# LayerNorm outputs transposed once in float32 and split behind the transpose, in a fused attention and ternary-FFN kernel

## The chip, the cores and the metric

The kernel runs on one core of one Trainium2 chip. The metric is the device time in microseconds; shown is the median of repeated runs. Engine names are those of the profile: PE is TensorE (matmuls; PEld is its weight load), DVE is VectorE, ACT is ScalarE, POOL is GpSimd, SP is the engine that issues the DMAs. Two kinds of 32-bit type occur: F32, and F32R[...].

## The reference

One transformer block on x of shape 8 x 1024 x 256. Attention has 16 query heads and 4 key/value heads of 16, so four query heads share a key head.

```python
x = L0_attn_x
x = x + _layernorm(attn(_layernorm(x), Wq, Wk, Wv, Wo))
x = x + _layernorm(ffn(_layernorm(x), weight, alpha, bias))

# attn(x): q, k, v = x @ Wq, x @ Wk, x @ Wv; rotary on q and k
#          p = softmax(q k^T / sqrt(256)); o = p v; return o @ Wo
# ffn(x):  w = ternary(weight) * alpha; return x @ w^T + bias
# _layernorm(x) = (x - mean) / sqrt(var + 1e-5), over the last axis
```

## The kernel before

**Units and stages.** The 8192 tokens are cut into 16 units of 512 (`UT` = 4 tiles of 128 rows, two units to a batch entry). A unit passes through three stages that belong to different units at any one time. `Project(u)` takes LayerNorm of x, transposes it, and makes q, k and v. The main loop computes scores and attention. `Tail(u)` multiplies by Wo, adds the residual, takes a second LayerNorm, runs the FFN and its LayerNorm, and stores. A stage works on halves of a unit, p = 0 and 1, each of two row tiles (128 x 512 numbers). The last unit has a tail of its own, `LastTail`, in four quarters.

**Precision.** To keep float32 accuracy with F32R matmuls, a LayerNorm output is split in two F32R parts, hi (the rounded value) and lo (the value less hi). `split_hi` is a tensor_scalar on POOL (line 157) or a copy on ACT (line 159), `split_lo` a subtraction (line 162). `product` (line 279) then adds up hi x hi, hi x lo and lo x hi, and the FFN product hi x w and lo x w. A matmul contracts over partitions, so both parts must be transposed: `transposed` (line 262) does four 128 x 128 transposes of one part into one PSUM bank and lets ACT copy the bank to SBUF.

**Main loop.** 2048 score groups `s` (512 steps of four, 32 steps to a unit) are done in windows (line 1114) of two or three. A window issues for each group a matmul `se` (line 655), whose result ACT exponentiates (line 671), and matmuls `sm` (line 582) for later groups, whose row maxima DVE takes (line 607). DVE reduces a pair of sm results in one wide instruction; where a window ends inside a pair, each half is reduced alone. Behind the scores stands at most one part of a stage that needs a PSUM bank, and then the `av` matmuls (line 691) of an earlier window. Of the scores' PSUM banks, se rotates through three, which the stage parts share.

**Order.** PE, DVE and ACT follow the order of the code in the main loop. POOL and SP are ordered by the planner when the kernel is built. The stages are lists of named parts with the step at which each falls due: `P_PARTS` (line 942) counts from SPU * (u - 4), with SPU = 32, and `T_PARTS` (line 953) from SPU * (u + 1); `P_FIRST` and `T_LAST` replace the steps for project 3 and for the tail of unit 14. So in loop unit U the tail of unit U - 1 and the projection of unit U + 3 run. Due parts queue in order in `ready`. A part that needs a bank (`banked`, line 1043) makes the window one of two groups, and only one such part is taken in it; parts behind it wait. Each run of 32 groups must be filled exactly, so a window of two may also come without a part:

```python
size = min(2 if s >= REGULAR and any(banked(*p) for p in ready) else 3, left, ends - s)
if left - size == 1:
    size += 1 if size == 2 else -1
```

**What the change touches.** `Project.begin` (line 341) takes the statistics (DVE and three small POOL instructions), normalizes (POOL) and splits (`hi`, `lo`, on POOL); `Project.x(p, l)` transposes part l of half p. Projects 0 to 2 call these methods one by one in the start-up lists. In the tail, `stats_x` (line 807) takes the statistics of x1, normalizes (`norm`) and splits (`split`); `Tail.x(p, l)` transposes; `ffn` multiplies. `shift_rows` (line 626) and `shift_low` (line 635) turn the score maxima of a block into rows of the queries, with tiles mh and ml.

Of the kernel before, what the change touches and what calls it, by code (L numbers as in the profile page):

```python
# [8 lines left out]
F32 = mybir.dt.float32  # L9
F32R = mybir.dt.float32r  # L10
# [6 lines left out]
P = 128  # L17
# [4 lines left out]
UT = 4  # L22
# [6 lines left out]
def kernel(  # L29
# [29 lines left out]
    nc = tc.nc  # L59
    B, S, D = x.shape  # L60
# [3 lines left out]
    ND = D // P  # L64
# [11 lines left out]
    work = ctx.enter_context(tc.tile_pool(name="work", bufs=2))  # L76
    qkp = ctx.enter_context(tc.tile_pool(name="qkp", bufs=1))
# [19 lines left out]
    ident = const.tile([P, P], F32, name="ident")  # L97
# [57 lines left out]
    def split_hi(eng, hi, src):  # L155
        if eng is nc.gpsimd:
            eng.tensor_scalar(hi, src, 1.0, 0.0, ALU.mult, ALU.add)
        else:
            nc.scalar.copy(hi, src)  # L159

    def split_lo(eng, lo, src, hi):
        eng.tensor_tensor(lo, src, hi.bitcast(F32), ALU.subtract)  # L162

    def split(eng, hi, lo, src, hi_eng=None):

        split_hi(hi_eng or eng, hi, src)
        split_lo(eng, lo, src, hi)
# [15 lines left out]
    def psum(shape, name, dtype=F32):  # L183
        if spare[0]:
            spare[0] += 1
            if spare[0] % 5 < 2:
                return ps_mx.tile(shape, dtype, tag="sm", name=name)
        return ps_e.tile(shape, dtype, tag="se", name=name)
# [4 lines left out]
    ffn = {}  # L193
# [37 lines left out]
    def ln_stats(src):  # L231

        n = src.shape[1]
        mv = small.tile([P, 2, 2], F32, tag="mv", name="mv")[:, :n]
        st = small.tile([P, 2, 6], F32, tag="bnst", name="bnst")
        for t in range(n):
            nc.vector.bn_stats(st[:, t, :], src[:, t, :])  # L237
        for t in range(n):
            nc.vector.bn_aggr(mv[:, t, :], st[:, t, :])  # L239
        sc = small.tile([P, 2, 2], F32, tag="lnsc", name="lnsc")[:, :, :n]  # L240
        nc.gpsimd.tensor_scalar(sc[:, 1, :], mv[:, :, 1], EPS, 1.0, ALU.add, ALU.mult)  # L241
        nc.gpsimd.tensor_tensor(sc[:, 1, :], sc[:, 1, :], mhalf[:, :n], ALU.pow)  # L242
        nc.gpsimd.tensor_scalar(sc[:, 0, :], mv[:, :, 0], -1.0, 0.0, ALU.mult, ALU.add)
        return mv, sc
# [17 lines left out]
    def transposed(src, tag, name, copy=nc.scalar.copy):  # L262

        pt = psum([P, ND, 2 * P], f"pt_{name}", F32R)
        for t in range(2):
            for c in range(ND):
                nc.tensor.transpose(  # L267
                    pt[:, c, t * P : (t + 1) * P], src[:, t, c * P : (c + 1) * P], ident_r
                )
        dst = work.tile([P, ND, 2 * P], F32R, tag=tag, name=name, bufs=2 if tag[0] == "x" else 1)  # L270
        copy(dst, pt.bitcast(F32))  # L271
        return dst

    TERMS = ((0, 0), (0, 1), (1, 0))

    def chunk(part, c):
        return part[c] if isinstance(part, list) else part[:, c]

    def product(out, left, right, terms=TERMS):

        steps = [(i, j, c) for i, j in terms for c in range(ND)]
        for k, (i, j, c) in enumerate(steps):
            nc.tensor.matmul(  # L283
                out,
                chunk(left[i], c),
                chunk(right[j], c),
                start=(k == 0),
                stop=(k == len(steps) - 1),
            )
# [15 lines left out]
    class Project:  # L305
# [3 lines left out]
        def __init__(self, u, eng):  # L309
            self.u, self.eng = u, eng  # L310
            self.b, self.half = divmod(u, UPB)
            self.xt, self.sc, self.hl = {}, {}, {}
            self.q_rot = None
            if u not in (1, 2):
                xn = qkp.tile([P, UT, D], F32, tag="xn", name=f"xn_{u}", bufs=2)
                xs = qkp.tile([P, 2, UT, D], F32R, tag="hl", name=f"xs_{u}")
                self.xn = [xn[:, 2 * p : 2 * p + 2, :] for p in range(2)]
                self.xs = [[xs[:, l, 2 * p : 2 * p + 2, :] for l in range(2)] for p in range(2)]
            else:
                self.xn = [  # L320
                    tailp.tile([P, 2, D], F32, tag=f"xn{p}", name=f"xn_{u}_{p}") for p in range(2)
                ]
                self.xs = [
                    [ep.tile([P, 2, D], F32R, tag="e", name=f"xs_{u}_{p}_{l}") for l in range(2)]
                    for p in range(2)
                ]
# [14 lines left out]
        def begin(self, p):  # L341
            self.stats(p)
            self.norm(p)
            self.hi(p)
            self.lo(p)

        def x(self, p, l):
            self.xt[p, l] = transposed(self.xs[p][l], f"xt{l}", f"xt{l}_{self.u}_{p}")

        def kv(self, p):  # L350

            if p == 0:
                self.pkv = psum([P, UQ], f"pkv_{self.u}")
            xt = [self.xt[p, l] for l in range(2)]
            product(self.pkv[:, self.tokens(p)], columns(wqkv_s, D, 2 * DK), xt)
            if p == 1:
                self.kv_t = qkp.tile([P, UQ], F32, tag="kv_t", name=f"kv_t_{self.u}")
                nc.scalar.copy(self.kv_t, self.pkv)
# [196 lines left out]
    def block_queries(i, r2=slice(None)):  # L555

        u, j = divmod(i, G)
        if u < NU - 1:
            return q_st[u % 2][:, j, r2, :]
        return q_st[u % 2][:, :, r2, j * P : (j + 1) * P]  # L560
# [65 lines left out]
    def shift_rows(i):  # L626

        m = mhl.pop(i)
        pm = psum([8 * UT, P], f"pm_{i}")
        nc.tensor.transpose(pm, m.rearrange("p a l x -> p (a l x)"), ident)  # L630
        mh = work.tile([8 * UT, P], F32R, tag="mh", name=f"mh_{i}")
        nc.scalar.copy(mh, pm)
        mhl[i] = pm, mh

    def shift_low(i):

        pm, mh = mhl.pop(i)
        ml = work.tile([8 * UT, P], F32R, tag="ml", name=f"ml_{i}")
        nc.vector.scalar_tensor_tensor(ml, mh.bitcast(F32), sels[3], pm, ALU.mult, ALU.add)
        n = 4 * UT  # L640
        for a in range(2):
            row = 64 * a + NROW
            dst = block_queries(i)[row : row + 2].bitcast(F32)
            if len(dst.shape) == 4:
                dst = dst.rearrange("l j c t -> l (j c) t")
            shifts[i] = nc.sync.dma_start(out=dst, in_=ml[n * a : n * a + n, :].bitcast(F32)).ins
# [68 lines left out]
    class Tail:  # L715
# [16 lines left out]
        def copy(self, p):  # L732
            return nc.scalar.copy
# [47 lines left out]
                self.copy(p)(hl[:, 0], self.on[p])  # L781
            split_lo(self.eng(p), hl[:, 1], self.on[p], hl[:, 0])

        def x(self, p, l):
            self.xt[p, l] = transposed(self.hl[p][:, l], f"ot{l}", f"ot{l}_{self.u}_{p}")

        def attn(self, p):
            pa = psum([P, self.width, D], f"pa_{self.u}_{p}")
# [18 lines left out]
        def stats_x(self, p):  # L807
            self.sc[p] = ln_stats(self.x1[p])
            self.norm(p)
            self.split(p)  # L810

        def stats_f(self, p):
            self.sc[p] = ln_stats(self.a[p])
# [24 lines left out]
    class LastTail(Tail):  # L838
# [54 lines left out]

        x = o

        def sa(self, p):
            self.sc[p] = ln_stats(self.a[p])

# [13 lines left out]
    def at(step, f, *args):  # L912
        assert step >= -START
        todo.setdefault(step, []).append((f, args))
# [22 lines left out]
    def load(u):  # L937
# [2 lines left out]


    P_PARTS = (
        (26, "begin", 0), (33, "x", 0, 0), (34, "x", 0, 1), (37, "begin", 1), (43, "x", 1, 0),
        (45, "x", 1, 1), (49, "kv_and_dram"), (51, "q", 0), (52, "kt"), (53, "v"), (55, "q", 1),
        (57, "q_to_dram"),
    )
    L_PARTS = (
# [5 lines left out]
    T_PARTS = (  # L953
        (1, "fetch"), (7, "invert"), (8, "scale", 0), (9, "scale", 1), (12, "attn", 0),
        (15, "attn", 1), (15, "stats_a", 0), (17, "stats_a", 1), (19, "stats_x", 0),
        (23, "stats_x", 1), (24, "x", 0, 0), (25, "x", 0, 1), (26, "ffn", 0), (27, "x", 1, 0),
        (29, "x", 1, 1), (31, "ffn", 1), (31, "stats_f", 0), (33, "stats_f", 1),
    )

    P_FIRST = (47, 51, 52, 54, 57, 58, 59, 60, 62, 61, 63, 64)  # L960
    T_LAST = (1, 3, 4, 5, 9, 10, 11, 14, 17, 20, 21, 21, 22, 24, 25, 26, 23, 27)

    warm = []

# [49 lines left out]
    for u in range(3, NU):  # L1014
        start = SPU * (u - 4)
        steps = P_FIRST if u == 3 else [k for k, *_ in P_PARTS]
        at(start + steps[0] - 6, load, u)
# [11 lines left out]
    for u in range(NU - 1):  # L1029
        start = SPU * (u + 1)  # L1030
        at(start + 1, begin_tail, u)
        steps = [k for k, *_ in T_PARTS] if u < NU - 2 else T_LAST
        for k, (_, *p) in zip(steps, T_PARTS):
# [9 lines left out]
    def banked(f, args):  # L1043

        return f in (shift_rows, threshold, transpose_ternary) or (
            f is part and args[2] in ("x", "q", "v", "kv_and_dram", "attn", "ffn", "n", "o")
        )

    REGULAR = 40
# [20 lines left out]
    def collect(n):  # L1070

        if due and due[0][0] <= maxima_by(4 * n + 4) // 4 - 1:
            i = due.pop(0)[1]
            ready.insert(0, (shift_rows, (i,)))
        ready.extend(todo.pop(n, ()))
# [200 lines left out]
```

## Time and profile before

| what | us |
|---|---|
| median of 3 runs (1642.08 to 1643.09) | 1642.32 |
| the profiled execution | 1642.63 |
| its span, first to last instruction | 1640.8 |
| se matmuls busy, 2048 | 705.5 |
| sm matmuls busy, 2048 | 748.4 |
| exponentials on ACT (line 671), 1996 of 602 ns | 1058.2 |
| maxima on DVE (line 607), 712 of 1216 ns and 592 of 680 ns | 1237.2 |
| transposes of LayerNorm outputs in Project (line 267), 256 of 259 ns | 33.6 |
| transposes in Tail (line 267), 240 of 253 ns | 31.2 |
| ACT copies of them (line 271), 66 + 64 of about 0.6 us | 76.9 |
| hi on POOL in Tail (line 157), 60 of 625 ns | 37.0 |
| lo on POOL in Tail (line 162), 60 of 1287 ns | 76.5 |
| mean granted TensorE clock, share of full | 0.989 |

The rows come from the groups of instructions: busy time, and how many of which mean length. The hi and lo rows of Tail hold also the splits of the attention output (`scale`). Half of the listed busy times overlap others: matmuls are pipelined, and row groups of PE run se and sm side by side, so PE's sums exceed what they take of the span.

### The profile page before, as it was taken

How to read it: one execution, taken by the hardware profiler on the slowest of the kernel's cores; microseconds unless marked ns; L12 is line 12 of the kernel's file. 1: busy time of each engine (PE TensorE's matmuls, PEld its weight loads, DVE VectorE, ACT ScalarE, POOL GpSimd, SP SyncE). 2: the span in 40 equal slices, each digit the busy share in tenths (PEclk: the TensorE clock that was granted, in tenths of full speed). 3: DMA queues.
4: the chain of work that ended last, by engine and by line, in shares of the span. 5: the costliest groups of instructions: out<-in, count | busy, mean ns of one | idle time of the engine just before them, and what ended most of it. 6: DMA issues, size and time to landing. Idle time of an engine off the chain costs nothing.

```text
span 1640.8 us, 37250 instructions
## 1 busy us (share of the span) xinstructions
PE 1579.7 (96%) x14712; PEld 818.5 (50%) x14712; DVE 1399.3 (85%) x2049; ACT 1274.8 (78%) x2479; POOL 835.4 (51%) x1239
## 2 busy tenths in 40 slices
PE   7999999999999999999999999999999999999997
PEld 5544455454545545454544545455454544444544
DVE  7778788889898888989889898988989888898964
ACT  4657778878787887878788787887878787877884
POOL 5532457374653737455373835547374552323363
PEclk8989999999999999999999999999999999999999
DMA  4151425125151422515133251513325151231100
GB/s 139 53 101 34 91 77 101 59 76 101 56 106 49 91 67 82 101 46 105 60 83 75 77 106 44 104 49 89 71 67 104 40 97 42 46 70 34 42 15 27
DMA packets 86079, 117.99 MB, mean 72 GB/s; under 512 B 12088, under 2 KB 50808, under 8 KB 85752
## 3 DMA queue, kind: packets, MB, share of 16 engines
q1 hardware_dynamic: 85904, 115.60, 29.9%
q8 instruction: 116, 1.90, 0.5%
q14 instruction: 59, 0.48, 0.1%
HBM read 68.65 MB, written 45.88 MB: 70 GB/s over the span
## 4 chain that ended last, share of the span: by engine, by line
PE 80%; DVE 10%; DMA 3%; ACT 2%; POOL 2%; issue 2%; SPq 1%; POOLq 0%; DVEq 0%; ACTq 0%
PE av L691 28%; PE se L655 28%; PE sm L582 9%; DVE mx L607 7%; PE pa L283 3%; PE pq L283 2%; PE pf L283 2%; PE pt_ot L267 2%; ACT e L671 2%; PE pt_xt L267 2%; PE pkv L283 2%; DMA q_st<-ml 1%; DMA k_rot<-d_k 1%; PE pm L630 1%; DMA dk<-ks 1%
## 5 line engine op out<-in xcount | busy, mean ns | idle before, releaser
L607 DVE TENSOR_REDUCE mx<-sm 128x2 f32<-128x1024 f32 (+1 forms) x1304 | 1205.3, 973 | 191.9 <-PE sm L582 174.1
L671 ACT ACTIVATE e<-se 128x512 f32<-128x512 f32 x1996 | 1058.2, 602 | 223.0 <-PE sm L582 172.4
L582 PE MATMUL sm<-k_st,q_st 64*128 64x512 f32 x2048 | 748.4, 450 | 6.9 <-DVE mx L607 3.9
L655 PE MATMUL se<-q_st,k_st 64*128 64x512 f32 x2048 | 705.5, 441 | 26.7 <-ACT e L671 14.4
L691 PE MATMUL av<-e,v_aug 128*32 128x256 f32 (+3 forms) x8608 | 607.2, 378 | 0.0
L655 PEld LDWEIGHTS se<-q_st,k_st 64*128 64x128 f32 x2048 | 324.9, 185 | 405.7 <-ACT e L671 302.1
L582 PEld LDWEIGHTS sm<-k_st,q_st 64*128 64x128 f32 x2048 | 326.1, 185 | 65.1 <-DVE mx L607 41.9
L691 PEld LDWEIGHTS av<-e,v_aug 128*32 128x32 f32 x8608 | 194.4, 108 | 211.0 <-issue 148.3
L241 POOL TENSOR_SCALAR lnsc<-mv 128x2 f32<-128x2 f32 (+1 forms) x134 | 25.8, 193 | 400.1 <-DVE mv L239 395.1
L765 POOL TENSOR_TENSOR xn<-xn,a 128x512 f32<-128x512 f32 x30 | 38.4, 1282 | 131.8 <-DMA a<-d_rec 101.2
L826 POOL TENSOR_TENSOR a<-a,bias_bc 128x512 f32<-128x512 f32 x30 | 38.6, 1287 | 108.3 <-ACT a L825 108.3
L242 POOL TENSOR_TENSOR lnsc<-lnsc,mhalf 128x2 f32<-128x2 f32 (+1 forms) x134 | 92.5, 691 | 0.9
L162 POOL TENSOR_TENSOR hl<-xn,hl 128x512 fp32r<-128x512 f32 x60 | 76.5, 1287 | 0.4
L253 POOL TENSOR_SCALAR xn<-x,lnsc 128x256 f32<-128x256 f32 x116 | 65.1, 570 | 2.2
L237 DVE BATCH_NORM_STATS2 bnst<-a 128x6 f32<-128x256 f32 x120 | 44.5, 413 | 4.6 <-POOL a L826 4.6
L297 POOL TENSOR_TENSOR t<-q_rot,sin_q_sb 128x512 f32<-128x512 f32 x31 | 39.9, 1288 | 15.5 <-ACT q_rot L439 15.4
L283 PE MATMUL pa<-woh,hl 128*128 128x256 f32 x240 | 46.2, 294 | 1.1 <-ACT e L671 1.1
L283 PE MATMUL pq<-xt,wqkvh 128*128 128x256 f32 x256 | 45.8, 303 | 0.5 <-ACT e L671 0.5
L237 DVE BATCH_NORM_STATS2 bnst<-x 128x6 f32<-128x256 f32 x124 | 45.9, 412 | 0.4 <-DMA x<-in_L_attn_x 0.4
L271 ACT CAST ot<-pt_ot 128x512 fp32r<-128x512 f32 x66 | 39.6, 601 | 4.7 <-PE pt_ot L267 4.7
L439 ACT COPY q_rot<-pq 128x512 f32<-128x512 f32 x32 | 18.8, 586 | 30.9 <-PE pq L283 30.9
L162 POOL TENSOR_TENSOR hlq<-q_rot,hlq 128x512 fp32r<-128x512 f32 x31 | 39.8, 1285 | 4.8 <-ACT hlq L159 4.5
(157 smaller groups left out, 1303.1 us busy)
## 6 DMA issues: line engine op xcount, KB each, us to landing
q_st<-dq SPq DMA_DIRECT2D x90, 256.0 KB
dq<-hlq SPq DMA_DIRECT2D x60, 256.0 KB
d_av<-avsb SPq DMA_DIRECT2D x60, 256.0 KB
x<-in_L_attn_x SPq DMA_DIRECT2D x15, 512.0 KB
xn<-d_av SPq DMA_DIRECT2D x30, 256.0 KB
a<-d_rec SPq DMA_DIRECT2D x30, 256.0 KB
xr<-in_L_attn_x SPq DMA_DIRECT2D x15, 512.0 KB
out_x<-a SPq DMA_DIRECT2D x30, 256.0 KB
```

What stands on the lines that cost most here:

```text
L162: eng.tensor_tensor(lo, src, hi.bitcast(F32), ALU.subtract)
L237: nc.vector.bn_stats(st[:, t, :], src[:, t, :])
L242: nc.gpsimd.tensor_tensor(sc[:, 1, :], sc[:, 1, :], mhalf[:, :n], ALU.pow)
L253: eng.tensor_scalar(dst[:, t, :], src[:, t, :], sc[:, 0, t : t + 1] if eng is nc.gpsimd else mv[:, t, 0:1], sc[:, 1, t : t + 1], ALU.add i ...
L267: nc.tensor.transpose(pt[:, c, t * P : (t + 1) * P], src[:, t, c * P : (c + 1) * P], ident_r)
L283: nc.tensor.matmul(out, chunk(left[i], c), chunk(right[j], c), start=(k == 0), stop=(k == len(steps) - 1),)
L297: eng.tensor_tensor(dst, x, table.unsqueeze(1).to_broadcast(list(x.shape)), ALU.mult)
L582: scores = nc.tensor.matmul(sm[0][:, part, :], queries[rows], k_st[(u // UPB) % 3][rows, r2, ch * 512 : (ch + 1) * 512], start=True, stop= ...
L607: early[0] = nc.vector.tensor_reduce(mx[i][:, a, head_and_tile(i, r2, t), lo:n], sm[0][:, lo:n, :], AX.X, ALU.max).ins
L655: nc.tensor.matmul(sc if len(queries.shape) == 2 else sc.rearrange("p (j t) -> p j t", j=G), k_st[(i // G // UPB) % 3][rows, r2, kt * P : ...
L671: nc.scalar.activation(e, sc, AF.Exp, scale=1.0 / D**0.5)
L691: nc.tensor.matmul(av_ps[0][32 * r : 32 * r + 32, lo:hi], va[:, kt, r, :], es[i * NK + kt, r // 2, r % 2][:, lo:hi], start=(kt == 0 and lo ...
```

## The change

A new helper transposes a half once, in F32 with the F32 identity, lets ACT copy the bank to one F32 tile, and splits that tile on POOL. Projects 3 to 15 and the tails of units 0 to 14 use it as a part `xw`, which takes the place of two parts `x`. The split before the transposes goes from `begin` and `stats_x`; `LastTail` keeps it. The tile xs is now made for project 0 alone (projects 1 and 2 have theirs elsewhere), mh and ml have one buffer in place of two, and the lists of steps are rewritten: in a tail, the transposes of half 0 fall due at 22, before the statistics of half 1.

```diff
+    def transposed_split(src, tag, name):
+        pt = psum([P, ND, 2 * P], f"pt_{name}")
+        for t in range(2):
+            for c in range(ND):
+                nc.tensor.transpose(
+                    pt[:, c, t * P : (t + 1) * P], src[:, t, c * P : (c + 1) * P], ident
+                )
+        whole = work.tile([P, ND, 2 * P], F32, tag=tag, name=name, bufs=1)
+        nc.scalar.copy(whole, pt)
+        parts = [
+            work.tile(
+                [P, ND, 2 * P], F32R, tag=f"{tag}{l}", name=f"{name}_{l}",
+                bufs=2 if tag[0] == "x" else 1,
+            ) for l in range(2)
+        ]
+        split(nc.gpsimd, *parts, whole)
+        return parts
...
         def begin(self, p):
             self.stats(p)
             self.norm(p)
-            self.hi(p)
-            self.lo(p)
...
+        def xw(self, p):
+            self.xt[p, 0], self.xt[p, 1] = transposed_split(self.xn[p], "xt", f"xt_{self.u}_{p}")
...
-        def x(self, p, l):
-            self.xt[p, l] = transposed(self.hl[p][:, l], f"ot{l}", f"ot{l}_{self.u}_{p}")
+        def xw(self, p):
+            self.xt[p, 0], self.xt[p, 1] = transposed_split(self.on[p], "ot", f"ot_{self.u}_{p}")
...
         def stats_x(self, p):
             self.sc[p] = ln_stats(self.x1[p])
             self.norm(p)
-            self.split(p)
...
     P_PARTS = (
-        (26, "begin", 0), (33, "x", 0, 0), (34, "x", 0, 1), (37, "begin", 1), (43, "x", 1, 0),
-        (45, "x", 1, 1), (49, "kv_and_dram"), (51, "q", 0), (52, "kt"), (53, "v"), (55, "q", 1),
+        (26, "begin", 0), (33, "xw", 0), (37, "begin", 1), (43, "xw", 1), (49, "kv_and_dram"), (51, "q", 0), (52, "kt"), (53, "v"), (55, "q", 1),
         (57, "q_to_dram"),
     )
...
-        (23, "stats_x", 1), (24, "x", 0, 0), (25, "x", 0, 1), (26, "ffn", 0), (27, "x", 1, 0),
-        (29, "x", 1, 1), (31, "ffn", 1), (31, "stats_f", 0), (33, "stats_f", 1),
+        (22, "xw", 0), (23, "stats_x", 1), (26, "ffn", 0), (27, "xw", 1), (31, "ffn", 1),
+        (31, "stats_f", 0), (33, "stats_f", 1),
     )
-    P_FIRST = (47, 51, 52, 54, 57, 58, 59, 60, 62, 61, 63, 64)
-    T_LAST = (1, 3, 4, 5, 9, 10, 11, 14, 17, 20, 21, 21, 22, 24, 25, 26, 23, 27)
+    P_FIRST = (47, 51, 54, 57, 59, 60, 62, 61, 63, 64)
+    T_LAST = (1, 3, 4, 5, 9, 10, 11, 14, 17, 19, 20, 22, 25, 27, 24, 28)
```

In `shift_rows` and `shift_low` the tiles mh and ml get `bufs=1`, `LastTail.stats_x` calls `split` behind the inherited method, and `banked` lists `xw`.

More of the change, by code (lines that the diff above doesn't have):

```diff
@@ L315, in __init__ @@
                 xn = qkp.tile([P, UT, D], F32, tag="xn", name=f"xn_{u}", bufs=2)
-                xs = qkp.tile([P, 2, UT, D], F32R, tag="hl", name=f"xs_{u}")
                 self.xn = [xn[:, 2 * p : 2 * p + 2, :] for p in range(2)]
-                self.xs = [[xs[:, l, 2 * p : 2 * p + 2, :] for l in range(2)] for p in range(2)]
+                if u == 0:
+                    xs = qkp.tile([P, 2, UT, D], F32R, tag="hl", name=f"xs_{u}")
+                    self.xs = [[xs[:, l, 2 * p : 2 * p + 2, :] for l in range(2)] for p in range(2)]
             else:
@@ L630, in shift_rows @@
         nc.tensor.transpose(pm, m.rearrange("p a l x -> p (a l x)"), ident)
-        mh = work.tile([8 * UT, P], F32R, tag="mh", name=f"mh_{i}")
+        mh = work.tile([8 * UT, P], F32R, tag="mh", name=f"mh_{i}", bufs=1)
         nc.scalar.copy(mh, pm)
@@ L637, in shift_low @@
         pm, mh = mhl.pop(i)
-        ml = work.tile([8 * UT, P], F32R, tag="ml", name=f"ml_{i}")
+        ml = work.tile([8 * UT, P], F32R, tag="ml", name=f"ml_{i}", bufs=1)
         nc.vector.scalar_tensor_tensor(ml, mh.bitcast(F32), sels[3], pm, ALU.mult, ALU.add)
@@ L894, with stats_x @@
         x = o
+        def stats_x(self, p):
+            super().stats_x(p)
+            self.split(p)
         def sa(self, p):
@@ L1045, in banked @@
         return f in (shift_rows, threshold, transpose_ternary) or (
-            f is part and args[2] in ("x", "q", "v", "kv_and_dram", "attn", "ffn", "n", "o")
+            f is part and args[2] in ("x", "xw", "q", "v", "kv_and_dram", "attn", "ffn", "n", "o")
         )
```

## The prediction

> **What bounds the kernel now.** I read the page first, then a table of the span cut into units, then the order of single instructions inside one unit.
>
> ```profile
> PE 1579.7 (96%) x14712; PEld 818.5 (50%) x14712; DVE 1399.3 (85%) x2049; ACT 1274.8 (78%) x2479; POOL 835.4 (51%) x1239
> ...
> PE av L691 28%; PE se L655 28%; PE sm L582 9%; DVE mx L607 7%; PE pa L283 3%; PE pq L283 2%; PE pf L283 2%; PE pt_ot L267 2%; ACT e L671 2%; PE pt_xt L267 2%; PE pkv L283 2%; DMA q_st<-ml 1%; DMA k_rot<-d_k 1%; PE pm L630 1%; DMA dk<-ks 1%
> ```
>
> TensorE (PE) is busy 96% and holds 80% of the chain of waits; the transposes that the change touches (pt_ot, pt_xt) are some 4% of it. But VectorE (DVE) is busy 85%, so I asked what a unit costs with less PE work. The units can be told apart by their score matmuls (128 groups each). Units 1 to 12 carry a tail and a projection, 13 and 14 a tail alone. One of each:
>
> ```profile
> core 0: us, PE busy (x) PEld busy (x) DVE busy (x) ACT busy (x) POOL busy (x), PEclk, DMA share, GB/s
> 662.80:759.10 96.30, 94.80 (x922) 48.76 (x918) 85.17 (x125) 78.29 (x153) 53.38 (x78) 1.00 0.34 79
> 1339.40:1432.30 92.90, 90.36 (x872) 44.35 (x868) 83.53 (x121) 74.21 (x145) 30.60 (x46) 1.00 0.25 54
> ```
>
> The busy PE of a row includes matmuls that stand waiting, so I worked out PE's own demand from the chain of waits in unit 6, where nothing else ends last:
>
> ```profile
> 670.41 0.43 PE se L655
> 670.84 0.23 PE sm L582 x2
> ...
> 671.07 0.23 PE sm L582
> 671.30 0.79 PE av L691 x16
> ...
> 672.75 0.46 PE pt_xt L267 x4
> 673.22 0.57 PE av L691 x8
> ```
>
> A window of three score pairs costs PE 0.43 + 0.23 + 0.23 + 0.79 = 1.68 us, one of two 0.43 + 0.23 + 0.57 = 1.23 us: about 0.33 us a window and 0.45 us a pair. Walked through the window rules of the code, unit 6 has 22 windows of two and 28 of three: 27.1 + 47.0 = 74.1 us. Its parts add 15.2 us, by their slots in the chain (12-matmul products 1.62 us, five of them; ffn 1.14, two; eight transpose groups 0.46; four pm about 0.22; one v about 0.3). Demand 89.3 us of 96.3. Unit 13 (13 and 34 windows, no projection) comes to 81.4 us of 92.9. So 7.9 us less PE work gave only 3.4 us: **the loop is PE-bound in part only**. In unit 13 the missing time is DVE's, whose wide reductions run 1.216 us a pair, and whose statistics come in bursts of 1.2 us (two of 0.41 and two of 0.17), during which PE's next sm waits.
>
> **The transposes.** From project 3 on (13 projects) and in 15 tails, two halves each, 56 pairs of fp32r groups become 56 single fp32 groups. The trace has both kinds:
>
> ```profile
> 672.68 0.53 PE L267 MATMUL pt_xt<-ident_r,xs 128*128 128x128 f32 x4
> 673.15 0.64 PE L691 MATMUL av<-e,v_aug 128*32 128x256 f32 x8
> ...
> 147.62 0.66 PE L225 MATMUL pt_w<-ident,up 128*128 128x128 f32 x4
> 148.20 0.42 PE L691 MATMUL av<-e,v_aug 128*32 128x256 f32 x4
> ```
>
> From the group's start to the next matmul: fp32r 673.15 - 672.68 = 0.47 us (0.462 finer), fp32 148.20 - 147.62 = 0.58 (0.587). Saved per half: 2 x 0.462 - 0.587 = 0.337 us; over 56 halves **18.9 us of PE**. The Trainium skill ("TensorE: Matmul & The Clock Gate", Part 4) prices a 128x128 transpose in a kernel at about 275 ns[...]: four fewer per half would be 1.1 us, 62 us in all. The rows agree with it as durations (253 to 259 ns fp32r, 286 fp32), but transposes overlap and PE's next work starts after 0.46; the slot decides, so 18.9, not 62.
>
> **The windows.** Each transpose group takes a two-pair window of its own. Walking the changed lists through the same rules, a regular unit goes from 22 and 28 windows to 19 and 30: one fewer, 0.33 us. Four groups vanish, but a block of 32 pairs must come out even, so one empty two-pair window comes back. PE demand per regular unit falls by 4 x 0.337 + 0.33 = 1.68 us.
>
> **ScalarE (ACT).** One 0.59 us copy per half goes (56, 33 us). ACT is busy 78 of 96 us in unit 6; its value is that PSUM score banks come free a little sooner. I count nothing of its own.
>
> **DVE.** No operation changes. Two more three-pair windows per unit split one more reduction in two: 2 x 0.68 - 1.216 = +0.14 us. DVE's 85.2 us a unit stay, so DVE is what is late next.
>
> **GpSimd (POOL).** The same two splits per half (0.62 and 1.28 us), moved behind the transpose. The Trainium skill ("GPSIMD Engine Reference", 4.1) speaks against this place: GpSimd has no way to PSUM. Hence the added link ACT copy, then POOL; where 0.6 us lay between transposes and product, 0.6 + 1.9 = 2.5 us now lie, plus both queues. POOL in unit 6 is full from 722 to 749; from its order of instructions and PE's (start, us, engine, line):
>
> ```profile
> 731.25 1.09 POOL L253 TENSOR_SCALAR xn<-x,lnsc 128x256 f32<-128x256 f32 x2
> ...
> 734.75 1.27 POOL L162 TENSOR_TENSOR hl<-xn,hl 128x512 fp32r<-128x512 f32 x1
> ...
> 738.51 0.53 PE L267 MATMUL pt_ot<-ident_r,hl 128*128 128x128 f32 x4
> ...
> 744.17 0.96 PE L283 MATMUL pf<-wt,ot 128*128 128x256 f32 x6
> ```
>
> Three places must hold:
> 1. The transpose of tail half 0 moves ahead of q 1, to about 734.2 in this unit's time (v at 729.3, its av, two three-pair windows, one pair of scores). Its input xn is ready at 732.3, or 733.1 as kv (which POOL's kt waits for by DMA) moves back a quarter step. Margin about 1 us.
> 2. ffn 0 keeps its slot at 744.2. Copy done about 736.2, split alone 738.1; with the norm of half 1 ahead of it (2.25 us) 740.4. Margin 4 us.
> 3. Half 1: the group stays at 750.3, copy about 752.2, split 754.1, ffn 1 at 757.4. Margin 3 us.
>
> In the projection the splits have from step 2 and 13 to kv at 18 (3.2 us a step): free. Queued behind a waiting split on POOL are q's rotation and the next norm; q goes to DRAM three units ahead, so that delay costs nothing. Behind PE's wait for a split stands everything.
>
> **Edits at nothing.** The single buffers of mh and ml are used once in some 24 us and their 8 KB transfer is short beside that. The wait of POOL's xs for the q tile's DMA (25.6 us in 9 waits) goes, but POOL then was ahead of need. q 1 a step later: q is used units later. The first project of the new kind has two steps (6.5 us) from its last transposes to kv and needs about 4.5: at worst a few us once.
>
> **The sum.** How much of 1.68 us arrives? All of it above: 1.7. Below, the mean of units 6 and 13, 3.4 / 7.9 = 0.43, and without DVE's own 1.6 us between them 0.26: 0.4 us. Between them the chain of waits decides. Cut to unit 6 it gives PE 94% and DVE 4%, cut to unit 13 DVE 17%: the first microsecond taken from PE counts nearly whole, the last of 7.9 nothing. A straight fall from 0.94 to 0 has about the mean seen (0.43 to 0.47), and over the first 1.68 us it averages 0.84: **1.4 us per regular unit, 17 us** in twelve. Units 13 and 14 give near 0.2 each (DVE-bound), unit 0 and unit 15 0.3 each. Together 18 us. The profiled execution took 1642.63 us, 1640.8 of it span; so 1622.8 of span and 1624.6. The median shown, 1642.32, lies 0.3 lower: **1624.5 us**.
>
> **Rivals.**
> - *PE alone bounds.* For it: 96% and the chain. A window taken out then counts by its mean from start to start: transpose windows 1.97 us (106 in the middle of the run), three-pair ones 1.77, empty ones 1.45. Per unit -4 x 1.97 + 4 x 0.125 + 2 x 1.77 + 1.45 = -2.4 us, some -25 to -30 us: 1615. Against: in unit 13 the three-pair windows have slowed to a mean of 1.90.
> - *DVE already bounds.* At 0.26 of PE's gain (-5 us) or less, with small new waits against it: 0 to -5 us, 1640. For it: DVE 85.2 of 96.3 busy, and bursts that transpose windows now cover. Against: DVE's 4% of the chain in unit 6.
> - *Slower: the split comes late for ffn 0.* POOL's order is fixed when the kernel is built. If q 1's rotation and split (6.0 us) are put ahead of the split along with the norm, it ends at 746.4, 2.2 us after PE wants it, in each of twelve units. It decides from a wait of 1.4 us a unit. Net 12 x (2.2 - 1.4) = +10 us: 1652; with place 1 late too, more. Against: the split is issued before q 1, and can start sooner.
> - That the groups aren't halved is excluded: the rewritten parts transpose xn itself.
>
> **How the numbers follow.** Forecast 0.47 (-10 to -23 us, own range 1619 to 1632), PE alone 0.20, DVE 0.15, late split 0.18. A change within 0.2% (3.3 us) can't be told from none. Faster: 0.47 + 0.20 + a third of the DVE case = 0.70; same 0.11; slower 0.19. The range 1611 to 1646 takes in most of the PE case, the DVE case and the edge of the late split.
>
> **What would show it.** Right: pt groups of 0.58 us, half as many; 30 windows of three in a regular unit; units near 95.2 us; three-pair windows slower than 1.77; DVE's share up to 86%. Wrong: PE waits at pf or pt_ot released by POOL of a microsecond or more in each unit (late split), units at 94.3 (PE alone) or unchanged (DVE).

## The result, and the profile after

| | before | after |
|---|---|---|
| median of 4 runs, us | 1642.24 | 1697.33 (1696.61 to 1698.52) |
| profiled execution, us | 1642.63 | 1696.64 |
| its span, us | 1640.8 | 1694.9 |
| mean granted TensorE clock | 0.989 | 0.972 |

The changed kernel is slower: ratio 1.0335, 95% interval 1.0317 to 1.0353, so 55 us, where 18 us less were forecast. Its page, busy times and chain of waits:

```profile
PE 1598.8 (94%) x14440; PEld 811.3 (48%) x14440; DVE 1398.7 (83%) x2054; ACT 1246.4 (74%) x2423; POOL 838.5 (49%) x1239
...
PE 59%; DVE 22%; DMA 9%; POOL 3%; issue 3%; SPq 2%; ACT 2%; POOLq 0%; ACTq 0%; DVEq 0%
PE av L712 21%; PE se L676 19%; DVE mx L628 18%; PE sm L603 8%; PE pa L302 3%; DMA q_st<-ml 2%; PE pq L302 2%; PE pf L302 2%; DMA dk<-ks 2%; DMA k_rot<-d_k 2%; PE pkv L302 1%; DVE bnst L237 1%; PE pt_ot L279 1%; DMA d_k<-kv_t 1%; ACT e L692 1%
```

PE does fewer matmuls (14440 for 14712) and is yet busy for 19 us more: a first hint that they ran slower. In the chain DMAs have gone from 3% to 9%, and two of them, `q_st<-ml` and `dk<-ks`, belong to steps that the change was not about. (The code has moved down by some 20 lines: se is L676, sm L603, the maxima L628, av L712. A float32 transpose is L279, a product L302.)

The loop cut into units again, unit 6, unit 10 and unit 13:

```profile
core 0: us, PE busy (x) PEld busy (x) DVE busy (x) ACT busy (x) POOL busy (x), PEclk, DMA share, GB/s
687.80:788.40 100.60, 96.16 (x906) 48.15 (x902) 85.06 (x125) 76.33 (x148) 53.67 (x78) 0.98 0.32 75
1091.00:1193.00 102.00, 97.33 (x904) 49.01 (x900) 85.10 (x125) 76.32 (x148) 53.65 (x78) 0.97 0.31 74
1397.60:1488.20 90.60, 88.07 (x840) 42.36 (x836) 82.14 (x119) 72.10 (x142) 30.64 (x46) 1.00 0.25 52
```

The loss is in the units with a projection: on average 101.1 us for 96.65 (units 2 to 12), and 107.8 for 99.2 in unit 1. Units 13 and 14, which have only the changed tail, won 2.4 and 1.5 us. And the granted clock of the slow ones is below 1. Each of units 2 to 12 has one gap on PE of more than 0.9 us, at its step 24 (the timeline of unit 9: start, us, engine, line, operation):

```profile
1058.30 0.64 PE L712 MATMUL av<-e,v_aug 128*32 128x256 f32 x8
1062.26 0.76 PE L676 MATMUL se<-q_st,k_st 64*128 64x512 f32 x1 [3.31 <-DMA q_st<-ml]
...
1063.41 1.11 PE L279 MATMUL pt_ot<-ident,xn 128*128 128x128 f32 x4
...
1067.04 1.03 PE L302 MATMUL pq<-xt,wqkvh 128*128 128x256 f32 x4
```

PE stands 3.31 us for the transfer of ml, the low parts of block 3's score maxima, and what follows takes 1.5 to 1.7 times its usual time (0.76 us for 0.50, 1.11 for 0.66). The same stretch in windows, clock in the third column from the right (before the DMA share and GB/s):

```profile
1050.00:1058.00 8.00, 7.60 (x83) 3.89 (x79) 6.14 (x7) 6.09 (x13) 7.50 (x13) 1.00 0.17 51
1058.00:1062.00 4.00, 0.94 (x11) 0.16 (x8) 1.92 (x3) 1.21 (x3) 3.37 (x5) 0.86 0.34 87
1062.00:1064.00 2.00, 1.74 (x7) 1.12 (x8) 0.48 (x1) 0.94 (x2) 0.00 (x0) 0.50 0.01 4
1064.00:1066.00 2.00, 2.00 (x21) 0.83 (x19) 0.74 (x1) 0.73 (x2) 0.68 (x2) 0.50 0.00 0
1066.00:1068.00 2.00, 2.00 (x9) 1.35 (x10) 0.82 (x1) 1.09 (x2) 1.22 (x1) 0.57 0.46 128
1068.00:1070.00 2.00, 2.00 (x19) 1.24 (x19) 1.28 (x5) 0.72 (x2) 0.28 (x1) 1.00 0.01 3
```

So a wait costs twice: PE runs at half clock for some microseconds behind it. All twelve units with a projection have the wait (2.0 to 3.3 us, 31 us together), and eleven have the half clock behind it, for 58 us together.

Why is the transfer late? It is SP's work, and SP issues in the planner's order. SP's queue in unit 9 of after:

```profile
1052.56 2.38 SPq L451 DMA_DIRECT2D dk<-ks  x4
1056.81 3.22 SPq L502 DMA_DIRECT2D k_st<-dk  x6
1060.13 1.41 SPq L667 DMA_DIRECT2D q_st<-ml  x2
```

and in unit 6 of before:

```profile
725.40 2.36 SPq L430 DMA_DIRECT2D dk<-ks  x4
728.69 3.35 SPq L481 DMA_DIRECT2D k_st<-dk  x6
732.14 1.41 SPq L646 DMA_DIRECT2D q_st<-ml  x2
```

In both the ten DMAs of kt stand ahead of ml's two. DVE had ml ready at 727.88 in before (its instruction began at 727.55 and took 0.33 us); its DMA was issued 4.3 us later, and the first se of step 24 began at 734.54, 6.7 us behind ml, without a wait. In after ml was ready at 1054.03 and its DMA was issued 6.1 us later; PE would have been at the same se at 1058.94 (end of av), 4.9 us behind ml. So 1.8 us are lost on SP, where kt's first DMAs go out 1.0 us later against ml and the second ones follow 1.0 us later behind them (4.25 us for 3.29). Another 1.8 us are lost on PE, since q 1 (1.62 us, 732.35 to 733.97 in before) no longer stands ahead of step 24: in after it begins at 1067.04.

In unit 6 of before the transfer just fitted. In six of the other units PE already waited 0.2 to 0.9 us for it at step 24. These waits stood in the trace before the change was made, small as they are. Over the whole run, start-up included (us in total, times, longest), before and after:

```profile
PE se L655 <- DMA q_st<-ml: 9.9, 8, 3.1
```

```profile
PE se L676 <- DMA q_st<-ml: 42.7, 16, 5.7
```

Unit 1, which lost the most, has a second wait of the kind at its step 8: 5.7 us, for 3.1 in before. There ml was ready at 192.75 in after, and SP issued its DMA 8.6 us later, for 4.0 us in before (194.56 to 198.55). In after two of the DMAs of project 3's q stand ahead of it, in before none:

```profile
197.40 0.63 SPq L763 DMA_DIRECT2D xn<-d_av  x1
198.12 1.21 SPq L493 DMA_DIRECT2D dq<-hlq  x2
199.38 1.89 SPq L768 DMA_DIRECT2D den<-d_av  x1
201.38 2.18 SPq L667 DMA_DIRECT2D q_st<-ml  x2
```

### The profile page after: what moved, and what is told of

Its sections match the earlier page's. It is cut to its first block, busy times and chain, and to the rows that moved or that the text cites. A ratio compares the mean times of both kernels' runs of the same rounds, so it can differ in the third digit from the quotient of the medians.

```text
span 1694.9 us, 36717 instructions
## 1 busy us (share of the span) xinstructions
PE 1598.8 (94%) x14440; PEld 811.3 (48%) x14440; DVE 1398.7 (83%) x2054; ACT 1246.4 (74%) x2423; POOL 838.5 (49%) x1239
## 4 chain that ended last, share of the span: by engine, by line
PE 59%; DVE 22%; DMA 9%; POOL 3%; issue 3%; SPq 2%; ACT 2%; POOLq 0%; ACTq 0%; DVEq 0%
PE av L712 21%; PE se L676 19%; DVE mx L628 18%; PE sm L603 8%; PE pa L302 3%; DMA q_st<-ml 2%; PE pq L302 2%; PE pf L302 2%; DMA dk<-ks 2%; DMA k_rot<-d_k 2%; PE pkv L302 1%; DVE bnst L237 1%; PE pt_ot L279 1%; DMA d_k<-kv_t 1%; ACT e L692 1%
## 5 line engine op out<-in xcount | busy, mean ns | idle before, releaser
L628 DVE TENSOR_REDUCE mx<-sm 128x2 f32<-128x1024 f32 (+1 forms) x1309 | 1205.2, 970 | 244.5 <-PE sm L603 191.3
L603 PE MATMUL sm<-k_st,q_st 64*128 64x512 f32 x2048 | 756.6, 453 | 16.6 <-DVE mx L628 7.7
L676 PE MATMUL se<-q_st,k_st 64*128 64x512 f32 x2048 | 721.7, 448 | 48.4 <-DMA q_st<-ml 42.7
L712 PE MATMUL av<-e,v_aug 128*32 128x256 f32 (+2 forms) x8560 | 612.1, 383 | 0.0
L676 PEld LDWEIGHTS se<-q_st,k_st 64*128 64x128 f32 x2048 | 330.0, 187 | 418.6 <-ACT e L692 240.2
L603 PEld LDWEIGHTS sm<-k_st,q_st 64*128 64x128 f32 x2048 | 329.1, 188 | 94.5 <-DVE mx L628 73.3
L712 PEld LDWEIGHTS av<-e,v_aug 128*32 128x32 f32 x8560 | 196.7, 109 | 233.6 <-issue 171.6
L157 POOL TENSOR_SCALAR ot<-ot 128x512 fp32r<-128x512 f32 x30 | 18.6, 621 | 83.9 <-ACT ot L283 63.7
L157 POOL TENSOR_SCALAR xt<-xt 128x512 fp32r<-128x512 f32 x26 | 16.2, 622 | 65.3 <-ACT xt L283 65.3
L302 PE MATMUL pq<-xt,wqkvh 128*128 128x256 f32 x256 | 47.9, 313 | 0.4 <-ACT e L692 0.4
L302 PE MATMUL pa<-woh,hl 128*128 128x256 f32 x240 | 46.2, 294 | 1.1 <-ACT e L692 1.1
L302 PEld LDWEIGHTS pq<-xt,wqkvh 128*128 128x128 f32 x256 | 38.3, 208 | 13.0 <-issue 11.6
```

The costliest lines, as they stand in the source:

```text
L302: nc.tensor.matmul(out, chunk(left[i], c), chunk(right[j], c), start=(k == 0), stop=(k == len(steps) - 1),)
L603: scores = nc.tensor.matmul(sm[0][:, part, :], queries[rows], k_st[(u // UPB) % 3][rows, r2, ch * 512 : (ch + 1) * 512], start=True, stop= ...
L628: early[0] = nc.vector.tensor_reduce(mx[i][:, a, head_and_tile(i, r2, t), lo:n], sm[0][:, lo:n, :], AX.X, ALU.max).ins
L676: nc.tensor.matmul(sc if len(queries.shape) == 2 else sc.rearrange("p (j t) -> p j t", j=G), k_st[(i // G // UPB) % 3][rows, r2, kt * P : ...
L712: nc.tensor.matmul(av_ps[0][32 * r : 32 * r + 32, lo:hi], va[:, kt, r, :], es[i * NK + kt, r // 2, r % 2][:, lo:hi], start=(kt == 0 and lo ...
```

## The experiments

**Theory A** is the one just told: the loss is the wait at step 24 and the half clock behind it, and both come from the order of kt, q 1 and ml, not from transposing in float32. Its rivals are worded in the expectations below. Each ratio is against runs of the kernel before on the same chip; its medians there lay between 1642 and 1648 us, so the ratios are what is compared.

### kt behind ml

kt falls due two steps later, behind v, and its DMAs may be issued only behind ml's of the same unit:

```diff
-        ... (51, "q", 0), (52, "kt"), (53, "v"), (55, "q", 1),
+        ... (51, "q", 0), (53, "v"), (54, "kt"), (55, "q", 1),
...
+    def kt_behind(u):
+        with tc.issue_after(shifts[4 * u - 9]):
+            projects[u].kt()
```

> The changed kernel; the key part kt falls due at 54 in place of 52, and its DMAs (dk<-ks, k_st<-dk) are queued on SP behind the transfer of the score maxima (q_st<-ml) of the block before; nothing else differs. Theory A (the maxima's transfer stands on SP behind the keys' DMAs, so PE waits about 2.7 us at step 24 of each of units 1 to 12, and then runs 3.4 or 6.8 us at half clock): the waits at step 24 and the half clock in units 2 to 12 go, 1622 us (1614 to 1634), units near 95.2 us. Theory B (the split behind the transpose comes late for the products): no effect, 1697. Theory C (float32 transposes themselves cost more than before): no effect, 1697.

Measured: 1642.62 us, ratio 0.9985 [0.9975, 0.9996]. SP's queue in unit 6, and the unit's row in the table of windows:

```profile
732.14 1.38 SPq L667 DMA_DIRECT2D q_st<-ml  x2
733.62 2.32 SPq L451 DMA_DIRECT2D dk<-ks  x4
736.91 4.67 SPq L502 DMA_DIRECT2D k_st<-dk  x6
```

```profile
666.90:763.30 96.40, 94.65 (x904) 47.51 (x900) 84.98 (x125) 76.20 (x149) 53.55 (x78) 1.00 0.34 78
```

With every transpose of the change in place, the wait at step 24 and the half clock behind it are gone and the 55 us with them: A holds for the loss, and the rivals B and C fall. But the gain that should then come to light did not: the unit takes 96.40 us, where 95.2 had been predicted and where undisturbed units of before take 96.3. That is a second question, taken up below.

### The tails alone, the projections alone

Before with `xw` in the tails alone (old `Project`, old `P_PARTS`), and after with the tails as they were:

```diff
# tails alone, from after
-            (33, "xw", 0), (37, "begin", 1), (43, "xw", 1),
+            (33, "x", 0, 0), (34, "x", 0, 1), (37, "begin", 1), (43, "x", 1, 0), (45, "x", 1, 1),
...
# projections alone, from after
-        (22, "xw", 0), (23, "stats_x", 1), (26, "ffn", 0), (27, "xw", 1), (31, "ffn", 1),
+        (23, "stats_x", 1), (24, "x", 0, 0), (25, "x", 0, 1), (26, "ffn", 0), (27, "x", 1, 0), (29, "x", 1, 1), (31, "ffn", 1),
```

> The kernel before, with the new transpose and split in the tails alone (with the tails' new steps, and single mh and ml); projections as before. By the window rules q 1 then stays ahead of step 24, the new group of half 0 taking the empty window. Theory A: no wait at step 24, 1630 us (1624 to 1638). Theory B: the tail has the least time between split and product, so most of the loss is here: 1670 or more. Theory C: 30 of 56 halves, about half of the loss: 1670.

> The changed kernel with the tails as before (their transposes in two parts, split ahead, old steps); projections new. By the window rules q 1 then falls behind step 24. Theory A: waits of 2 us or more at step 24 and half clock behind them, slower than before: 1680 us (1660 to 1700). Theory B: the projection's splits have many steps, so no loss: 1630 to 1640. Theory C: 26 of 56 halves, 1667.

Tails alone: 1649.47 us, 1.0026 [1.0013, 1.0039], slower than the 1624 to 1638 us that A gave. Projections alone: 1702.62 us, 1.0356 [1.0324, 1.0388], the whole loss. The wait at step 24 is there in the second (2.2 to 4.2 us in each of the twelve units) and not in the first. The first, though, gained nothing. It has a wait that the prediction had listed as its first place (us in total, times, longest):

```profile
PE pt_ot L279 <- POOL xn L253: 13.6, 12, 1.5
```

In each unit with a projection PE comes to the moved transposes some 1.1 us before POOL has the normalized half. In after they come only behind the wait of step 24, and nothing of POOL's is missing then. And the two runs say what moves q 1. With the tails alone it stays ahead of step 24, with the projections alone it falls behind it. So what moves it is that the projection lost two transpose windows, by which its later parts fall on other windows, and not the tail's new part.

### One number in the kernel before

If A is right, the loss must come without any transpose changed:

```diff
-        ... (52, "kt"), (53, "v"), (55, "q", 1),
+        ... (52, "kt"), (53, "v"), (56, "q", 1),
```

> The kernel before with one number changed: q 1 of the projection falls due at 56 in place of 55, so that it comes behind step 24; the transposes stay as they were. Theory A: 1.6 us of cover are taken from the maxima's transfer, so PE waits 1 to 2 us at step 24 in units 1 to 12, with half clock behind the waits if they are long enough: 1660 us (1648 to 1690). Theories B and C: no change, 1642 within 4.

Measured: 1673.64 us, 1.0178 [1.0154, 1.0202], for an edit that the prediction priced at nothing. PE's timeline in unit 6, and the row of the waits over the run (us in total, times, longest):

```profile
748.83 0.46 PE L655 MATMUL se<-q_st,k_st 64*128 64x512 f32 x1 [2.20 <-DMA q_st<-ml]
```

```profile
PE se L655 <- DMA q_st<-ml: 33.6, 16, 4.0
```

q 1 one step later is enough to uncover the transfer in all twelve units (1.0 to 3.9 us, 22 us of the 29 lost; the other 7 are not accounted for). Only one of these waits, of 3.9 us, had the half clock behind it, so this run shows the wait nearly by itself.

### A filler in the wait

To weigh the half clock, fourteen matmuls of 384 columns into a PSUM bank of the kind that the parts use were put at step 24 of units 1 to 12 of after; nobody reads them:

```diff
+            if s % 128 == 96 and 1 <= s // 128 <= 12:
+                keep = psum([P, UQ], f"keep_{s}")
+                for _ in range(14):
+                    nc.tensor.matmul(keep[:, :QKV], ident_r, wqkv_s[0][:, 0, :], start=True, stop=True)
```

> The changed kernel with 14 matmuls of 384 columns that nobody reads, put ahead of the scores at step 24 of units 1 to 12, so that PE runs through most of the 2.7 us in which it waits for the maxima's transfer; the transfer is as late as before. If the half clock behind the wait costs time of its own: about 20 us less than the changed kernel, 1677 us (1668 to 1687), with no half clock in units 2 to 12. If the wait alone is the cost: no change, 1697 to 1702.

Measured: 1676.84 us, 1.0187 [1.017, 1.0205]. PE's timeline in unit 9, then the windows:

```profile
1050.93 2.74 PE L1150 MATMUL keep<-wqkvh,ident_r 128*128 128x384 f32 x14
1054.62 0.47 PE L676 MATMUL se<-q_st,k_st 64*128 64x512 f32 x1 [0.95 <-DMA q_st<-ml]
```

```profile
1050.00:1054.00 4.00, 3.67 (x25) 2.62 (x24) 1.98 (x3) 1.27 (x3) 2.99 (x5) 1.00 0.25 71
1054.00:1056.00 2.00, 1.38 (x12) 0.88 (x16) 0.61 (x1) 0.88 (x2) 0.00 (x0) 1.00 0.02 5
1056.00:1058.00 2.00, 2.00 (x25) 1.27 (x22) 1.16 (x2) 1.50 (x4) 1.14 (x2) 1.00 0.18 22
```

The se begins no earlier (3.6 us behind the end of av, for 3.3), but the clock stays at 1.00 (last columns again: clock, DMA share, GB/s): work that nobody reads made the kernel 1.5% faster. This splits the loss. From after to the filler, 1.0335 - 1.0187 = 1.48%, is the **half clock: 24 us**. From the filler to kt behind ml, 1.0187 - 0.9985 = 2.0%, is the **wait itself: 33 us** (2.7 us in each of twelve units). What is left of the change, 0.9985 - 1, is -0.15% or **-2.5 us**. Together 55.

The split is good to some microseconds only. By the intervals of the ratios the half clock's share can be off by 4 us. The filler also made the delay before se longer, 2.96 us for 2.62 on average or 4 us over the run, so the wait's share is rather too high and the half clock's too low. The traces agree: the waits of after sum to 31 us, and 58 us at half clock can cost PE at most 29.

### Where the 18 us went: DVE, or PE's order?

The other question starts from kt behind ml. **Theory D**: DVE bounds, so less of DVE's work must show at once. In both kernels LayerNorm takes the statistics of one tile of two and uses them for both, which takes away half of DVE's statistics (62 for 124 on x, 60 for 120 on a; 33 us with their aggregates):

```diff
-        for t in range(n):
-            nc.vector.bn_stats(st[:, t, :], src[:, t, :])
-        for t in range(n):
-            nc.vector.bn_aggr(mv[:, t, :], st[:, t, :])
+        nc.vector.bn_stats(st[:, 0, :], src[:, 0, :])
+        for t in range(n):
+            nc.vector.bn_aggr(mv[:, t, :], st[:, 0, :])
```

> The kernel of e1_kt_behind, in which every LayerNorm over two row tiles takes the statistics of its first tile for both (the second bn_stats of each pair is left out, so the second tile is normalized with the first one's numbers): 8 x 0.41 = 3.3 us less VectorE work in a regular unit, nothing less on PE. Theory D (with the waits gone, VectorE bounds the regular unit, and so PE's saving did not arrive): 2 to 3.3 us less in each of 14 units, 1600 us (1594 to 1612). Theory P (the saving was lost on PE or in waits for POOL): 0 to 1 us a unit, 1636 (1628 to 1642).

> The same cut of the statistics in the kernel before (the second tile of each pair is normalized with the first one's statistics). Theory D: before, PE led the chain in the regular units and VectorE only in units 13 and 14, so less than there: 0.5 to 1.5 us a unit, 1630 us (1622 to 1638). Theory P: 0 to 1 us a unit, as in the other kernel.

With kt behind: 1638.73 us, 0.994 [0.9921, 0.9959]; from before: 1634.12 us, 0.9915 [0.9895, 0.9934]. Unit 6 of the first:

```profile
667.70:763.80 96.10, 94.61 (x904) 47.45 (x900) 82.79 (x117) 76.18 (x148) 53.85 (x78) 1.00 0.35 79
```

DVE has 2.2 us less to do in it and the unit is 0.3 us shorter; units 13 and 14 won 0.8 and 0.7 us. So D falls for the kernel with kt behind: there DVE's sum doesn't bound the regular unit. For the kernel before this is not settled. Its 14 us lie in the range that either theory had named, and its profiled execution, 1640.98 us, was the slowest of four (the others took 1632.3 to 1635.4), so its trace doesn't show where they came from.

Two more runs frame the question: before with kt behind ml alone, to have the same base, and the changed kernel with kt behind and each group of transposes done twice into the same bank:

```diff
-        for t in range(2):
+        for t in (0, 1, 0, 1):
```

> The kernel before, with the key part's DMAs queued on SP behind the maxima's transfer as in e1_kt_behind; transposes as they were. Theory A: the transfer was covered before, so little: 1640 us (1636 to 1643), the 0.5 to 1 us that a few units longer than 96.3 show. Then what the change itself is worth without the late transfer is the difference to e1_kt_behind, 0 to 5 us. If the queue cost time in the kernel before too: 1632 or less.

> The kernel of e1_kt_behind with each new group of four float32 transposes done twice into the same bank: 4 x 0.44 = 1.75 us more PE work in a regular unit, which gives back what the change saves on PE, with the same windows, copies and splits. Theory D: PE's work is covered, 0 to 0.5 us a unit, 1643 us (1640 to 1650). If PE bounds: 1.4 us a unit, 1660 or more.

The first: 1641.55 us, 0.997 [0.9956, 0.9984], units at 96.3. The second: 1666.27 us, 1.0115 [1.01, 1.013], units at 98.15, as unit 6:

```profile
677.35:775.50 98.15, 96.38 (x922) 49.25 (x918) 85.19 (x125) 76.56 (x149) 53.51 (x78) 1.00 0.33 77
```

Four doubled groups of 0.43 us make 1.72 us, and the unit grew by 1.75. So PE's work *within* a transpose window counts in full. What did not count, in the regular units, was taking windows away.

The last pair tests that. It is after, with its float32 transposes, but with before's lists: where the second `x` stood, an empty part `gap` takes a two-pair window of its own, in the tail as shown and in the projection alike. Once with kt as in after, once behind ml:

```diff
-        (22, "xw", 0), (23, "stats_x", 1), (26, "ffn", 0), (27, "xw", 1), (31, "ffn", 1),
+        (23, "stats_x", 1), (24, "xw", 0), (25, "gap"), (26, "ffn", 0), (27, "xw", 1), (29, "gap"), (31, "ffn", 1),
```

> The changed kernel with the old steps: each new group stands where the first of the two old ones stood, and where the second stood a part that does nothing but claims a bank, so that every window has the size it had before (22 of two and 28 of three in a regular unit), q 1 stays ahead of step 24, and half of the old transpose windows are empty. Theory W (PE's saving was given back in the windows: eight score groups a unit that had ridden in transpose windows must be done elsewhere): by the window means of the kernel before, 4 x (1.97 + 0.125) + 4 x 1.45 in place of 8 x 1.97, 1.6 us less in each of 12 units, less what the split's wait at ffn 0 takes (POOL has q 1's split ahead of it: 0 to 1 us a unit): 1630 us (1620 to 1640), ratio 0.993, units 94.8 to 95.8 us. If the saving is lost whatever the windows: units 96.3 or more, 1642.

> e10_windows_as_before with the key part's DMAs queued on SP behind the maxima's transfer. Theory A and W together: as e10_windows_as_before, 0 to 4 us less: 1628 us, ratio 0.991, faster than the kernel before and than e1_kt_behind.

Measured: 1638.37 us, 0.996 [0.9947, 0.9972], and 1637.75 us, 0.9957 [0.9945, 0.9969]: each short of what was expected (0.993 and 0.991), but the fastest that compute the whole. They are faster than before and than the changed kernel with kt behind (0.9985). Against before with kt behind (0.997) the intervals overlap, and it is the units that differ. Unit 6 of the second:

```profile
664.00:759.70 95.70, 93.97 (x905) 47.64 (x902) 85.11 (x124) 76.26 (x149) 53.68 (x78) 1.00 0.35 79
```

95.7 for 96.3 us: 0.6 of the 1.35 us that the groups save (4 x 0.337). Of what is missing, 0.46 us a unit stand in the window of ffn 0, 3.19 us for 2.73 in before, where the weight loads of its product now wait for POOL's split:

```profile
PEld pf L302 <- POOL ot L162: 9.1, 14, 1.9
```

The wait of the sm matmuls for the bank that DVE's maxima free, over the run, tells the kinds of list apart. Before, the changed kernel with kt behind, and the same with windows as before:

```profile
PEld sm L582 <- DVE mx L607: 41.9, 127, 1.4
```

```profile
PEld sm L603 <- DVE mx L628: 73.8, 192, 1.4
```

```profile
PEld sm L606 <- DVE mx L631: 44.6, 146, 1.4
```

A table of window means, from the first se of one to the first se of the next, in units 2 to 12, shows the same per unit:

| kind of window | before | changed, kt behind |
|---|---|---|
| with a transpose group | 8 x 1.97 = 15.73 | 4 x 2.21 = 8.85 |
| three pairs | 28 x 1.766 = 49.44 | 30 x 1.787 = 53.61 |
| two pairs, no part | 2 x 1.449 = 2.90 | 3 x 1.710 = 5.13 |
| with v | 1.47 | 2.36 |

6.9 us less in the first row, 7.3 more in the others; q, kv and the rest give some 0.6 back. A transpose window also carries two score groups. The eight groups of four lost windows must go elsewhere, and there sm comes to its bank before DVE has emptied it. So the windows with transposes had given DVE time to catch up. The chain of waits says the same: DVE holds 10% of it in before, 23% in the changed kernel with kt behind, and 9% with windows as before.

Units 13 and 14, without a projection, went the other way: 92.9 us each in before, 90.6 and 91.4 in the changed kernel with kt behind, but 92.2 with windows as before. There taking windows away paid 1.6 and 0.8 us. Why it pays there and not in a regular unit no run shows.

## Why the prediction was wrong, point by point

- **"q 1 a step later: q is used units later"** (under "Edits at nothing") is the step that failed, with 57 of the 73 us between forecast and result. It put the delay at nothing because it asked who reads q and not what q 1 covered: on PE it stood between ml and the scores that need it. What leaned on its time was block 3's ml, issued behind ten DMAs of kt, with 6.7 us from ml to se. kt was named only as a thing that kv moves back, at place 1 on POOL; its DMAs on SP were not counted. And q 1's place is set by the windows ahead of it: two transpose windows fewer put it behind step 24. Measured price: 33 us of waits, and 24 us of half clock for which the sum had no term.
- **"The single buffers of mh and ml ... 8 KB transfer is short"**: the transfer is short, but its place in SP's queue decided, not its size or its buffer: with single buffers throughout, kt behind ml has no wait at step 24.
- **"The sum", 1.4 us per regular unit**: a second step that failed, hidden under the first. "Walking the changed lists" gave 19 and 30 windows, which came so, and the group's slot, 0.58 us on average with kt behind, is as read. But PE's demand, 1.35 us for the groups and 0.33 for one window fewer, times 0.84, gave 1.4 us a unit, where the unit took 96.4 us for 96.3: nothing arrived. What fits the runs: PE time within a window counts (1.75 of 1.72 us when doubled, 0.6 of 1.35 when saved, with 0.46 more lost to POOL's split). In a regular unit the windows taken away cost more than they brought, 96.4 us for 95.7 with the gaps in their place, since their score groups need DVE's time wherever they stand. Units 13 and 14, priced at near 0.2 us each as DVE-bound, won 2.4 and 1.5 us, together more than the 2.5 us that the change brought over the whole run without the late transfer. (A slip without weight: 1624.6 less 0.3 is 1624.3.)
- **DVE**: "DVE is what is late next" was right as to the engine (chain 10% before, 23% with kt behind) and wrong as to the quantity. What came late was not DVE's sum but its answer to an sm in a window without other PE work. The rival "DVE already bounds" named 0 to -5 us, which is what kt behind ml shows; its reason, DVE's sum, fell there with the halved statistics, so the number was right by luck.
- **"PE alone"** (windows by their means, -2.4 us a unit) failed on the same point: the means of the windows that stay went up.
- **"The split comes late for ffn 0"** did not happen in after: in its whole run the weight loads of pf wait 4.7 us for POOL, and places 2 and 3 held. With windows as before it did, at 0.46 us a unit. So the slower rival had the right sign for after by luck, since its place was the wrong one.
- **Place 1**, "margin about 1 us": none, as the tails alone show (12 waits of about 1.1 us).

## What to carry to other kernels

Before a part is moved past a point in the order, list what becomes ready just before that point and is needed just behind it, with the queue that carries it: an edit is free only if no such transfer leaned on its time. Where a queue is ordered by a planner, look at it for small urgent DMAs behind bulky ones, and pin the order; here one ordering rule, with kt due two steps later, was worth 3.5% of the run. Small waits for a transfer in the trace before, like the 0.2 to 0.9 us here, are a sign that it has no slack. And in a loop whose windows couple several engines, price what is taken out by its own slot within the window that stays, and don't count on a gain from taking the window away: here it cost 0.7 us in a regular unit and paid 0.8 to 1.6 us in units 13 and 14.

## What the hardware showed

The granted clock falls after a single wait of PE and comes back by itself: behind the waits at step 24 it is 0.50 for 3.4 or 6.8 us. By the length of the wait the edge is not sharp. In after, in the projections alone and in before with q 1 later, every wait of 2.6 us and more at step 24 brought the half clock (17 of 17). Of those between 1.9 and 2.6 us five of eleven did (2.08 us did in after's unit 2, 2.18 us in its unit 7 did not), and of those from 0.9 to 1.8 us none of eight. In the tails alone one of 1.3 us did, and one of 3.1 us in before, at step 8 of unit 1, did not. The Trainium skill ("TensorE: Matmul & The Clock Gate", "Why this matters for your kernels") asks for no gaps of PE above about 3 us between bursts; here gaps from 2 us on were often enough.

The clock records of the traces say more. In each trace all stretches of half clock begin on one even grid of 3.41 us. So it is the idle time within one interval of this grid that tells. In units 1 to 12 of all thirteen traces, the next interval ran at half clock in 30 of 30 cases where PE had idled 1.7 us or more of an interval at full clock, in 5 of 13 with 1.3 to 1.7 us, and never with less. The wait of 3.1 us in before lay across a grid line, with 1.5 us of idle time on one side and 1.6 on the other. A wait's place on the grid thus helps to decide what it costs; no run moved it on purpose.

Work that nobody reads kept the clock as well as work that counts.

Left open: each kernel waits for ml at step 8 of unit 1 (3.1 us in before, 3.4 to 4.1 in the others with the old projections, 5.3 to 6.8 with the new ones), and in the other traces unit 1 took 2 to 9 us longer than the 99.2 of before. The DMAs ahead of ml are shown above, but no run put them behind it. Why units 13 and 14 gained by the windows taken away is not known. Nor was it tried to put POOL's split ahead of q 1's where windows are as before.
